# Four-direction selective scan: tiles of two channels by 512 tokens become tiles of one channel by 1024 tokens

## The chip, the cores and the metric

The kernel runs on one core of a Trainium2 chip. A core has five engines with queues of their own: TensorE (PE, with its weight loads PEld), VectorE (DVE), ScalarE (ACT), GpSimd (POOL) and SyncE (SP), which here issues all DMAs. The metric is the device time of one execution in microseconds, lower is better.

## The reference, cut to what matters

The program is four layers of a vision network on a batch of B = 4 images with 96 channels of 64 x 64 pixels: a convolution with a selective scan in four directions (layer 0), an inverted-bottleneck convolution (layer 1), a spectral mixing layer with a feed-forward (layer 2), and linear attention with a feed-forward (layer 3). Nearly all of the time lies in the scan of layer 0, and the change touches that alone. Its core:

```python
K, N, R, DIN, DI = (4, 16, 6, 96, 192)      # directions, states, rank, channels in, channels
L = h * w                                   # 4096 tokens
xs = jnp.stack([xf, xt, jnp.flip(xf, -1), jnp.flip(xt, -1)], axis=1)
xdbl = jnp.einsum('bkdl,ked->bkel', xs, sel_w)
dts_r = xdbl[:, :, :R]
Bs = xdbl[:, :, R:R + N]
Cs = xdbl[:, :, R + N:]
delta = jax.nn.softplus(jnp.einsum('bkrl,kdr->bkdl', dts_r, dt_w) + dt_b[None, :, :, None])
A = -jnp.exp(A_logs.astype(jnp.float32)).reshape(K, DI, N)
def step(hst, inp):
    ut, dt_, bt, ct = inp
    dA = jnp.exp(dt_[..., None] * A[None])
    hst = hst * dA + (dt_ * ut)[..., None] * bt[:, :, None, :]
    y = jnp.einsum('bkdn,bkn->bkd', hst, ct)
    return (hst, y)
```

So for each image and direction there are 192 channels x 16 states = 3072 recurrences along 4096 tokens: decay exp(delta A), input delta u B, then the state times C, summed over the 16 states.

## The kernel before, in words

**Tiling.** The tokens are cut into NCH = 8 chunks of CH = 512. A step is one image, one direction and one chunk, 128 steps in all; its chunks run backwards in directions 2 and 3. A step has PC = 12 units. A unit takes 64 channels and 4 states: its 128 partitions are 32 channel pairs x 4 states, and its free dimension is 2 channels x 512 tokens (index e in the code). `PASSES` is ((0, 1), (2,)): first the channel groups 0 and 1, for each of the NJ = 4 groups of states, then group 2. So there are 1536 units.

**One unit** goes through these functions of `scans`:

- `inputs` (L1264): GpSimd multiplies `rep_g` (delta times u, every channel repeated over 4 partitions) with B (the first half of the tile `rep_BC`, broadcast over e) into a tile `db`, 128 x 1024.
- `decays` (L1268): for e = 0 and 1, ScalarE takes exp of `rep_d` times a column of A into a PSUM bank `da` (128 x 512). There are four such banks, two units' worth. Ahead of each exp stands the state copy `keep` (L1292) of the unit two slots back.
- `states` (L1278): DVE runs two scans of 512 tokens (L1285), from the state kept by the same unit of the step before, or from 0.0 in a direction's first step. In a unit listed in `POOL_C` the scans write an SBUF tile `hc`, otherwise they write over `da`. In the latter case two DVE products with C (L1290) follow, into `hc`.
- `product` (L1304): for a unit of `POOL_C`, (1, 3, 5, 7, 10) of 12, GpSimd copies the last states (L1302) and multiplies `hc` in place with C (L1306), two slots after the scan.
- `sums` (L1319): for two units together PE adds up the 4 states with four matmuls onto the quarters of a PSUM bank `y` (L1330), four slots after the second unit. `sums_out` (L1339) copies the bank by ScalarE (L1344) and stores it.

**What sets the order.** Everything in `scans` stands in an order written by hand for all five engines. The loop over slots (L1361), one unit a slot, emits in this order: loads of coming tiles, pending stores (`flush`), the exp of the next unit, the copy of a finished `y`, GpSimd's input of the unit after next, GpSimd's product of the unit two slots back, this unit's scans and products, the sums that are due, and then side work. Side work is all the rest of the network, cut into streams of small steps with estimated costs (`WORK`, `SHARE`, `RATE`); `advance` (L1451) gives each slot as much of it as its budget allows, in program order behind the slot's scan. `need` (L1245) makes sure that the inputs of the next step are traced, and runs side steps at once by `force` (L1470) until they are. When the scans are over, the streams that are left run alone, with all eight PSUM banks (`alone`, L1489).

**Inputs from DRAM.** `scan_inputs` (L578) computes delta (L610 to L623, stored from `z`), delta times u (L619, stored from `g`) and B, C (stored from `xd`) for each chunk and writes them to DRAM (`d_delta`, `d_du`, `d_bc`). `LOADS` (L1252) says at which unit each tile of the next step is loaded, repeated over partitions: three `rep_d`, three `rep_g`, four `rep_BC` a step, each of 512 KB with runs of 4 KB. `SCAN` gives the numbers of buffers: 3, 3, 5, and 4 `db`, 7 `hc`.

**Around it.** `turn` (L629) and `scan_outputs` (L671) read the results `d_y` once `scanned` says that enough chunks are through; `scan_outputs` ends in L736 and L738, and the convolution of layer 1 (`conv_block`, L742) follows it, chunk pair by chunk pair. For the last image the last direction is 2, backwards, so its chunks are finished in the order 7 to 0, and layer 1 starts while the scan still runs. Side work takes its SBUF tiles from rings: `tmp` (TMP = 10 tiles) and `arrival` (IN = 5).

Of the kernel before, what the change touches and what calls it, by code (L numbers as in the profile page):

```python
# [19 lines left out]
F32 = mybir.dt.float32  # L20
# [8 lines left out]
L = H * W  # L29
# [5 lines left out]
NCH = L // CH  # L35
RPC = CH // W
# [7 lines left out]
SCAN = {"rep_d": 3, "rep_g": 3, "rep_BC": 5, "db": 4, "hc": 7}  # L44
POOL_C = (1, 3, 5, 7, 10)
LAST = {"tab": 24, "more": 6}
TMP, IN = 10, 5

PC = NI * NJ // 2
PAIRS = K * NCH * PC  # L50

# [44 lines left out]
def hybrid_kernel(ctx: ExitStack, tc: tile.TileContext, a: dict):  # L96
# [16 lines left out]
    BANKS = {"mm": 3, "da": 4, "y": 1}  # L113
# [6 lines left out]

    def bank(tag="mm", turn=True):

        if alone and tag == "mm" and turn:
            tag = turns(alone)
        if tag == "mm":
            held_banks[0] += 1
        return psum.tile([128, CH], F32, name=f"ps_{tag}", tag=tag, bufs=BANKS[tag])

# [60 lines left out]
    def pair(tag):  # L189
        return sp.tile([128, 2, CH], F32, name=tag, tag=tag, bufs=SCAN[tag])  # L190

# [25 lines left out]

    d_delta = [images(f"delta{k}_", [NCH, DI, CH], sets=3) for k in range(K)]
    d_du = [images(f"du{k}_", [NCH, DI, CH], sets=3) for k in range(K)]
    d_bc = [images(f"bc{k}_", [NCH, 2 * NS, CH], sets=3) for k in range(K)]  # L220

    d_y = [images(f"y{k}_", [NCH, 256, CH]) for k in range(K)]
# [353 lines left out]
    def scan_inputs(b, u, o, c, done):  # L578
# [16 lines left out]
        for e in (0, 1):  # L595
            later(d_bc[o + 2 * e][i][c], xd[64 * e : 64 * e + 2 * NS])
        for part in range(3):
            yield pe(0.9, 1, part > 0)
            p = bank()
            if part < 2:  # L600
                mm(p, lhsT=dtw[:, o + 2 * part, 0:128], rhs=xd, start=True, stop=True)  # L601
                at = [(slice(0, 128), o + 2 * part, slice(0, 128))]
# [16 lines left out]
            nc.vector.tensor_mul(split(g), split(p), view(ub if part == 2 else ua, o, c))  # L619
            for rows, k, ch in at:  # L620
                later(d_du[k][i][c][ch], g[rows])
# [3 lines left out]
            for rows, k, ch in at:  # L625
                later(d_delta[k][i][c][ch], z[rows])
# [44 lines left out]
    def scan_outputs(b, done):  # L671
# [3 lines left out]
        def fetch(c):  # L675
            out = []
            yt, y0, y2 = (of[b % 2][c] for of in (d_yt, d_y[0], d_y[2]))
            for part in (yt[:128], y2[:128], yt[128:], y2[128:]) + ((y0[128:],) if b == B - 1 else ()):
                s = arrival("ypart")
                load(s[: part.shape[0]], part)  # L680
                out.append(s[: part.shape[0]])
# [508 lines left out]
    PASSES = ((0, 1), (2,))  # L1190
# [17 lines left out]
    def scans(stages):  # L1208
# [8 lines left out]
        for b in range(B):  # L1217
            for k in KORDER[b]:
                for n in range(NCH):
                    steps.append({"b": b, "k": k, "c": NCH - 1 - n if k >= 2 else n, "n": n, "BC": {}, "d": {}, "g": {}})  # L1220
        units = []
        for number, step in enumerate(steps):
            step["at"] = number % (K * NCH)
# [8 lines left out]
        def load_states(step, j):  # L1232
            t = pair("rep_BC")
            of = d_bc[step["k"]][step["b"] % 3][step["c"], 8 * j : 8 * j + 8].rearrange("(s e) l -> s (e l)", e=2)
            load(t.rearrange("p e l -> p (e l)"), of.unsqueeze(0).to_broadcast([32, 4, 2 * CH]))
            step["BC"][j] = t

        def load_channels(step, i, name):
            t = pair(f"rep_{name}")
            of = (d_delta if name == "d" else d_du)[step["k"]][step["b"] % 3][step["c"], 64 * i : 64 * i + 64]  # L1240
            load(t.rearrange("p e l -> p (e l)"),
                 of.rearrange("(p e) l -> p (e l)", e=2).unsqueeze(1).to_broadcast([32, 4, 2 * CH]))
            step[name][i] = t

        def need(step):  # L1245

            while (step["k"] % 2, step["c"]) not in traced[step["b"]]:
                force(stages)
# [394 lines left out]
```

## Time and profile before

| | |
|---|---|
| median of 3 runs | 6344.4 us (6340.63 to 6344.61) |
| profiled execution | 6358.61 us |
| its span, first to last instruction | 6356.8 us |
| first scan, last scan | about 81 us, about 5912 us |
| DMA | 1100.47 MB, mean 173 GB/s, 54.3% of 16 engines' span |

The slices of the span, 40 equal parts of 159 us, a digit being tenths of busy time:

```profile
PE   6732767756888776686469878767898777679998
DVE  4979898998999989989989998888999999889245
ACT  5743777765666677877546656767666667666435
POOL 4857878779999899987899998898999988889100
```

A line of instruction groups in this document reads: code line, engine, operation, output<-inputs with shapes, count, then busy us in total and mean ns of one, then the engine's idle time just before them and which instruction ended it ("<-"). A line of the order of time reads: start in us, length in us (of all instructions merged into the line, their number behind the x), engine, code line, operation. A line of busy time by stretch gives the stretch and its length, then the busy us (and instructions) of PE, PEld, DVE, ACT and POOL, and then the granted TensorE clock, the share of the DMA engines and GB/s.

### The profile page before, as it was taken

The page shows a single profiled execution, that of the slowest core. Times are in us where ns is not written, and L with a number is a line of the kernel's source. Part 1 is how long each engine was busy: PE and PEld are TensorE (multiplying, and loading weights), DVE is VectorE, ACT ScalarE, POOL GpSimd, SP SyncE. Part 2 cuts the span into 40 slices and gives each one's busy share as a digit, 9 for nine tenths or more (in the row PEclk, how much of TensorE's full clock was granted, in tenths as well). Part 3 has the DMA queues.
Part 4 walks back from the last instruction along what each step waited for, and adds up shares of the span by engine and source line. Part 5 has one row for each costly group of instructions (what it writes and reads, how often), then busy time and mean ns, then how long its engine had stood idle before and what let it go on. Part 6 is the DMA issues. An engine that isn't in the chain of part 4 may idle for free. (4 is left out here: it accounts for less than half of the span.)

```text
span 6356.8 us, 84759 instructions
## 1 busy us (share of the span) xinstructions
PE 4685.7 (74%) x27692; PEld 1723.3 (27%) x27692; DVE 5490.6 (86%) x6059; ACT 4191.3 (66%) x8072; POOL 5169.6 (81%) x2743
## 2 busy tenths in 40 slices
PE   6732767756888776686469878767898777679998
PEld 2100212201222642121012236321222552112274
DVE  4979898998999989989989998888999999889245
ACT  5743777765666677877546656767666667666435
POOL 4857878779999899987899998898999988889100
PEclk9855978867998888797779987878899887789999
DMA  5654565667754554456776445456754554566201
GB/s 178 206 167 146 190 204 187 201 201 221 221 162 151 183 181 156 151 193 208 212 213 197 156 152 192 157 162 199 225 171 159 171 192 141 172 209 202 84 13 39
DMA packets 430397, 1100.47 MB, mean 173 GB/s; under 512 B 74138, under 2 KB 75904, under 8 KB 428804
## 3 DMA queue, kind: packets, MB, share of 16 engines
q1 hardware_dynamic: 429956, 1095.06, 54.3%
q8 instruction: 220, 3.60, 0.2%
q14 instruction: 221, 1.81, 0.1%
HBM read 861.88 MB, written 237.44 MB: 173 GB/s over the span
## 5 line engine op out<-in xcount | busy, mean ns | idle before, releaser
L1266 POOL TENSOR_TENSOR db<-rep_g,rep_BC 128x1024 f32<-128x1024 f32 x1536 | 3607.0, 2365 | 689.1 <-DVE hc L1285 323.5
L1276 ACT ACTIVATE ps_da<-rep_d,aneg 128x512 f32<-128x512 f32 x3072 | 2061.8, 690 | 478.8 <-DVE hc L1285 347.2
L1285 DVE TENSOR_TENSOR_SCAN ps_da<-ps_da,state,db 128x512 f32<-128x512 f32 x1568 | 1923.9, 1272 | 274.3 <-ACT state L1300 151.4
L1306 POOL TENSOR_TENSOR hc<-hc,rep_BC 128x1024 f32<-128x1024 f32 x640 | 1511.2, 2361 | 49.3 <-DVE hc L1285 4.5
L1285 DVE TENSOR_TENSOR_SCAN hc<-ps_da,state,db 128x512 f32<-128x512 f32 x1120 | 1371.7, 1266 | 71.3 <-issue 20.6
L1330 PE MATMUL ps_y<-hc,cst 128*32 128x512 f32 x6144 | 1014.4, 739 | 566.2 <-POOL hc L1306 261.1
L1290 DVE TENSOR_TENSOR hc<-ps_da,rep_BC 128x512 f32<-128x512 f32 x1792 | 1135.5, 675 | 0.0
L1300 ACT COPY state<-ps_da 128x1 f32<-128x1 f32 x1568 | 246.3, 157 | 456.9 <-DVE hc L1290 455.4
L1330 PEld LDWEIGHTS ps_y<-hc,cst 128*32 128x32 f32 x6144 | 145.8, 118 | 1210.5 <-issue 438.2
L810 PE MATMUL ps_mm<-h,wd 128*32 128x512 f32 x3120 | 357.0, 593 | 7.0 <-ACT r L155 7.0
L550 PE MATMUL ps_mm<-xp,taps 128*128 128x512 f32 x576 | 294.7, 656 | 54.9 <-ACT ua L552 15.1
L1285 DVE TENSOR_TENSOR_SCAN ps_da<-ps_da,db 128x512 f32<-128x512 f32 x224 | 261.3, 1212 | 39.5 <-ACT state L1300 24.7
L787 PE MATMUL ps_mm<-wd,w 128*32 128x512 f32 x1984 | 254.9, 630 | 29.3 <-DMA wd<-x 20.0
L601 PE MATMUL ps_mm<-xd,dtw 128*128 128x512 f32 x256 | 168.5, 751 | 73.6 <-ACT z L623 53.5
L791 ACT ACTIVATE h<-ps_mm 128x512 f32<-128x512 f32 x261 | 151.8, 597 | 66.5 <-PE ps_mm L787 64.5
L869 PE MATMUL ps_mm<-r,cst 128*128 128x512 f32 x222 | 152.3, 778 | 56.5 <-ACT acc L892 14.2
L616 DVE SCALAR_TENSOR_TENSOR ps_mm<-ps_mm,z 128x512 f32<-128x512 f32 x192 | 131.7, 686 | 70.8 <-ACT z L614 67.0
L1285 DVE TENSOR_TENSOR_SCAN hc<-ps_da,db 128x512 f32<-128x512 f32 x160 | 186.2, 1204 | 6.1 <-issue 3.1
L655 PE MATMUL ps_mm<-ya,cst 128*64 128x512 f32 x192 | 183.1, 1044 | 10.4 <-ACT acc L892 10.4
L610 ACT ACTIVATE z<-ps_mm 128x512 f32<-128x512 f32 x192 | 114.1, 595 | 111.7 <-PE ps_mm L601 59.2
L982 PE MATMUL ps_mm<-wa,xp 128*64 128x96 f32 x1728 | 134.9, 318 | 64.6 <-DVE d L987 61.9
L550 PEld LDWEIGHTS ps_mm<-xp,taps 128*128 128x128 f32 x576 | 115.9, 208 | 229.5 <-issue 159.9
(348 smaller groups left out, 6675.9 us busy)
## 6 DMA issues: line engine op xcount, KB each, us to landing
rep_BC<-bc SPq DMA_DIRECT2D x512, 512.0 KB
rep_g<-du SPq DMA_DIRECT2D x384, 512.0 KB
rep_d<-delta SPq DMA_DIRECT2D x384, 512.0 KB
y<-yt SPq DMA_DIRECT2D x512, 128.0 KB
du<-g SPq DMA_DIRECT2D x128, 256.0 KB
delta<-z SPq DMA_DIRECT2D x128, 256.0 KB
tab<-in_etab SPq DMA_DIRECT2D x112, 256.0 KB
ya<-y SPq DMA_DIRECT2D x24, 1024.0 KB
```

Source lines behind the costliest of these rows:

```text
L550: mm(p, lhsT=taps[:, t, 0:128], rhs=window(t, c + e), start=t == 0, stop=t == 8)
L601: mm(p, lhsT=dtw[:, o + 2 * part, 0:128], rhs=xd, start=True, stop=True)
L655: mm(split(p[:64]), lhsT=const("two")[:, :64], rhs=t[:, :L].rearrange("p (w h) -> p h w", h=H)[:, c * RPC : (c + 1) * RPC, :], start=True, ...
L787: mm(p[32 * n : 32 * n + 32], lhsT=w1[:, 32 * g : 32 * g + 32], rhs=xin[:, n : n + 15 : 2, 1 : W + 1], start=True, stop=True)
L810: mm(p[32 * n : 32 * n + 32], lhsT=held["wd"][:, groups[i], o, dx, :], rhs=here[i][:, :, dx : dx + W], start=dx == 0, stop=dx == 2)
L1266: nc.gpsimd.tensor_mul(x["db"], x["step"]["g"][x["i"]], both(x["step"]["BC"][x["j"]][:, 0]))
L1276: act(x["da"][e], x["step"]["d"][x["i"]][:, e], AF.Exp, scale=aneg[:, av : av + 1])
L1285: nc.vector.tensor_tensor_scan(x["h"][e][:, order], x["da"][e][:, order], x["db"][:, e, order], start, ALU.mult, ALU.add)
L1290: x["made"] = nc.vector.tensor_mul(x["hc"][:, e], x["h"][e], x["step"]["BC"][x["j"]][:, 1])
L1300: nc.scalar.copy(to[:, e : e + 1], x["h"][e][:, end : end + 1])
L1306: x["made"] = nc.gpsimd.tensor_mul(x["hc"], x["hc"], both(x["step"]["BC"][x["j"]][:, 1]))
L1330: done = mm(y[32 * q : 32 * q + 32], lhsT=const("stack"), rhs=x["hc"][:, e], start=first or (x["pass"] == 0 and x["j"] == 0), stop=last or ...
```

## The change

The unit keeps its 128 x 1024 elements, and there are still 1536 of them, but it is cut otherwise: 32 channels (no pairs) x 4 states on the partitions, and 1024 tokens of one channel on the free dimension. What follows from that:

- A step covers 1024 tokens: 64 steps of PC = 24 units, in three passes of two channel groups. `need` asks for both chunks of a step.
- One exp of 1024 elements writes a tile of two PSUM banks; there are two such tiles instead of four single banks. One scan of 1024 takes the place of two of 512, one DVE product of 1024 that of two.
- The input, the state (in units whose product GpSimd makes) and the product are written in place in one tile `w` from a ring of 8; `db` (4) and `hc` (7) are gone. A `w` tile is free again when the sums of its unit are done.
- `POOL_C` becomes (0, 2, 4, 6, 8, 12, 14, 16, 18, 20) of 24; GpSimd's product stays two slots behind the scan. All state copies are ScalarE's, one column each.
- B and C are loaded as tiles of their own, four of each a step, beside six `d` and six `g`, each with 4 buffers; `LOADS` and `OWN` place these loads anew. The DRAM tensors hold 1024 tokens a row; B and C are no longer interleaved.
- The sums come three slots after the second unit (four before). They still take four matmuls for two units; now the halves of a bank are the two chunks.
- TMP goes from 10 to 9, IN from 5 to 4, the ring of `yt` to 1. `scan_outputs` packs two half loads into one tile.
- When the scans are over, `bank("da")` hands out halves of the two-bank tiles in turn. `force` gives banks back when no stream fits.

The diff, cut to its core:

```diff
-SCAN = {"rep_d": 3, "rep_g": 3, "rep_BC": 5, "db": 4, "hc": 7}
-POOL_C = (1, 3, 5, 7, 10)
+SCAN = {"d": 4, "g": 4, "B": 4, "C": 4, "w": 8}
+POOL_C = (0, 2, 4, 6, 8, 12, 14, 16, 18, 20)
-TMP, IN = 10, 5
-PC = NI * NJ // 2
+TMP, IN = 9, 4
+PC = NI * NJ
-    BANKS = {"mm": 3, "da": 4, "y": 1}
+    BANKS = {"mm": 3, "da": 2, "y": 1}
...
+    def decay_banks():
+        return psum.tile([128, CH2], F32, name="ps_da", tag="da", bufs=BANKS["da"])
...
-    PASSES = ((0, 1), (2,))
+    PASSES = ((0, 1), (2, 3), (4, 5))
...
+        def fetch(step, name, i):
+            t = step[name][i] = wide(name)
+            if name in "BC":
+                lo = 4 * i + (NS if name == "C" else 0)
+                of = d_bc[step["k"]][step["b"] % 3][step["c"], lo : lo + 4].unsqueeze(0)
+            else:
+                of = (d_delta if name == "d" else d_du)[step["k"]][step["b"] % 3]
+                of = of[step["c"], 32 * i : 32 * i + 32].unsqueeze(1)
+            load(t, of.to_broadcast([32, 4, CH2]))
...
-            while (step["k"] % 2, step["c"]) not in traced[step["b"]]:
+            while not traced[step["b"]].issuperset((step["k"] % 2, 2 * step["c"] + e) for e in (0, 1)):
                 force(stages)
...
-        LOADS = {4: [("BC", 0)], 5: [("g", 0)], 6: [("g", 1), ("d", 0)], 7: [("d", 1)], 10: [("BC", 1), ("g", 2)],
-                 11: [("BC", 2), ("d", 2)], PC + 1: [("BC", 3)]}
+        LOADS = {14: [("g", 0)], 15: [("g", 1), ("d", 0)], 16: [("d", 1), ("B", 0)], 18: [("B", 1)], 20: [("B", 2), ("C", 0)],
+                 21: [("C", 1)], 22: [("g", 2), ("B", 3)], 23: [("g", 3), ("d", 2)]}
+        OWN = {0: [("C", 2), ("d", 3)], 2: [("C", 3)], 6: [("g", 4)], 7: [("g", 5), ("d", 4)], 8: [("d", 5)]}
...
         def inputs(x):
-            x["db"] = pair("db")
-            nc.gpsimd.tensor_mul(x["db"], x["step"]["g"][x["i"]], both(x["step"]["BC"][x["j"]][:, 0]))
+            x["w"] = wide("w")
+            nc.gpsimd.tensor_mul(x["w"], x["step"]["g"][x["i"]], x["step"]["B"][x["j"]])
...
+            if last is not None:
+                keep(last)
+            av = (x["step"]["k"] * NI + x["i"]) * NJ + x["j"]
+            x["da"] = decay_banks()
+            act(x["da"], x["step"]["d"][x["i"]], AF.Exp, scale=aneg[:, av : av + 1])
...
+            x["h"] = x["w"] if x["pool"] else x["da"]
+            start = 0.0 if step["n"] == 0 else steps[x["number"] - 1]["last"][:, u : u + 1]
+            nc.vector.tensor_tensor_scan(
+                x["h"][:, order], x["da"][:, order], x["w"][:, order], start, ALU.mult, ALU.add
+            )
             if not x["pool"]:
-                for e in (0, 1):
-                    x["made"] = nc.vector.tensor_mul(x["hc"][:, e], x["h"][e], x["step"]["BC"][x["j"]][:, 1])
+                product(x, nc.vector)
...
+        def product(x, engine):
+            x["made"] = engine.tensor_mul(x["w"], x["h"], x["step"]["C"][x["j"]])
...
-            when = at + 4
+            when = at + 3
```

## The prediction

> **What bounds the kernel now.** I read the page's busy times first, then busy time by stage, then the groups of the scan, then a stretch of the vector engine's order of time, and last what its scans waited for.
>
> ```profile
> PE 4685.7 (74%) x27692; PEld 1723.3 (27%) x27692; DVE 5490.6 (86%) x6059; ACT 4191.3 (66%) x8072; POOL 5169.6 (81%) x2743
> ```
>
> By stage (span, then busy PE, PEld, DVE, ACT, POOL):
>
> ```profile
> 600.00:1500.00 900.00, 591.58 (x1851) 162.62 (x1852) 819.90 (x896) 640.43 (x1218) 729.51 (x388) 0.79 0.61 196
> 1500.00:2000.00 500.00, 418.34 (x2270) 115.45 (x2274) 470.21 (x502) 325.09 (x653) 494.05 (x264) 0.90 0.61 188
> 5915.00:6357.00 442.00, 410.24 (x4134) 231.11 (x4130) 164.20 (x301) 181.13 (x285) 0.00 (x0) 0.98 0.14 43
> ```
>
> The scans run from about 81 to 5912 us. In the first line, a stage with much side work, DVE is busy 91% and POOL 81%: DVE is the bound. In the second POOL is at 99%, yet DVE is at 94%: both bind. The last line is the tail without scans, PE at 93%. The groups of the scan:
>
> ```profile
> L1266 POOL TENSOR_TENSOR db<-rep_g,rep_BC 128x1024 f32<-128x1024 f32 x1536 | 3607.0, 2365 | 689.1 <-DVE hc L1285 323.5 <-DVE ps_da L1285 154.5 <-DMA rep_BC<-bc 116.8
> L1276 ACT ACTIVATE ps_da<-rep_d,aneg 128x512 f32<-128x512 f32 x3072 | 2061.8, 690 | 478.8 <-DVE hc L1285 347.2 <-DVE hc L1290 86.1 <-DMA rep_d<-delta 9.7
> L1285 DVE TENSOR_TENSOR_SCAN ps_da<-ps_da,state,db 128x512 f32<-128x512 f32 x1568 | 1923.9, 1272 | 274.3 <-ACT state L1300 151.4 <-ACT ps_da L1276 51.0 <-POOL db L1266 38.2
> L1306 POOL TENSOR_TENSOR hc<-hc,rep_BC 128x1024 f32<-128x1024 f32 x640 | 1511.2, 2361 | 49.3 <-DVE hc L1285 4.5
> L1290 DVE TENSOR_TENSOR hc<-ps_da,rep_BC 128x512 f32<-128x512 f32 x1792 | 1135.5, 675 | 0.0
> L1300 ACT COPY state<-ps_da 128x1 f32<-128x1 f32 x1568 | 246.3, 157 | 456.9 <-DVE hc L1290 455.4
> L1302 POOL COPY state<-hc 128x2 f32<-128x2 f32 x560 | 105.8, 189 | 0.0
> ```
>
> A mean overstates what an instruction costs its engine, since neighbours overlap. So I take distances between starts (start, us, count behind the x):
>
> ```profile
> 1244.22 0.69 DVE L616 SCALAR_TENSOR_TENSOR ps_mm<-ps_mm,z 128x512 f32<-128x512 f32 x1
> 1244.95 0.69 DVE L619 TENSOR_TENSOR g<-ps_mm,ub 128x512 f32<-128x512 f32 x1
> 1245.55 2.46 DVE L1285 TENSOR_TENSOR_SCAN ps_da<-ps_da,state,db 128x512 f32<-128x512 f32 x2
> 1247.92 1.27 DVE L1290 TENSOR_TENSOR hc<-ps_da,rep_BC 128x512 f32<-128x512 f32 x2
> 1249.10 0.69 DVE L616 SCALAR_TENSOR_TENSOR ps_mm<-ps_mm,z 128x512 f32<-128x512 f32 x1
> ```
>
> Two scans take 2.37, two products 1.18, an instruction after an unrelated one of 0.69 comes after 0.60, but L619, which reads what L616 has just written, comes after 0.73: a dependent neighbour costs 0.13 more. Last, what the scans of L1285 waited for (us, times):
>
> ```profile
>   ACT state L1300: 178.4, 114
>   ACT ps_da L1276: 66.0, 44
>   POOL db L1266: 57.3, 43
>   POOL hc L1306: 33.2, 16
> ```
>
> So DVE waits far longer for a late exp (244 us, 158 times) than for GpSimd (about 100 with 9 for L1302).
>
> [...]
>
> **The change part by part.** There are 1536 units before (128 steps of 12) and after (64 of 24), each of the same elements, and the products are split alike: 640 by GpSimd (P units), 896 by DVE (N units).
>
> *Scans and products on DVE.* One scan of 1024 replaces two. [...] a P unit saves 0.12. [...] But before, the order was scan, scan, product, product, with an instruction between each scan and its product; now the product directly follows its own scan and pays the 0.13. An N unit takes 2.25 + 0.13 + 1.13 = 3.51 against 3.55, saving about 0.05. Sum: 640 x 0.12 + 896 x 0.05 = 77 + 45 = **122 us gained** (from 5 without any fixed part on the scan to 240 without the wait). It lies on the path in all stages, if GpSimd follows.
>
> *GpSimd.* Its operands keep their size, 2.32 between starts. The copies of L1302 go: 560 x 0.27 = 151 us of POOL, of which I count nothing by itself; it lets GpSimd fall from 3.37 to 3.28 us a unit, faster than DVE's 0.08 a unit, so that in the second stage above the gain isn't stopped. The floor, 2176 x 2.32 = 5050 us in a zone of 5831, isn't reached.
>
> *State copies.* All go to ScalarE, one a unit, three steps of four: 1536 x 3/4 = 1152 instead of 1568. The in-place product now waits for that copy; GpSimd's queue behind it holds the inputs of later units, which have two slots of lead. Nothing.
>
> *Exp, and two decay tiles of two banks.* [...] 0.18 less of ACT a unit. But before, DVE could begin after the first half (0.69), and ACT could refill the first bank while DVE used the second. Now a scan waits for the whole 1.12, and the exp for the whole tile. Where ACT is already late, each time costs 0.43 more: 158 x 0.43 = 68. Near misses of today: 158 waits of 1.5 us mean suggest some 45 new ones of about 0.3, 14. Two slots of lighter ACT return 0.2 each time, 32. Net **50 lost** (from -32 to 165).
>
> *Loads.* As many of 512 KB as before (1280). B now leads its use by six slots where rep_BC led by two or three (issued at 10, 11 and 13, used from slot 12), so the 117 us that POOL waited for rep_BC should go; it reached DVE only as part of the 100, **25 gained** (0 to 60). In SP's queue each load sits one slot or two behind the last reader of its buffer, as before; stores queue behind it as they do now.
>
> *Ring w of eight.* It replaces 4 + 7 tiles. GpSimd's input of slot s+2 needs the sums of unit s-6, issued on PE at slot s-2 or earlier; DVE then has its two slots of lead. DVE's waits for ps_y today are 6.7 us in all. Nothing (0 to 30 lost).
>
> *Side buffers.* TMP 10 to 9, IN 5 to 4. Today waits for stores of z or g are about 2 us, but the buffers come round in some 19 us and are held for 15 to 20. **15 lost** (0 to 60).
>
> *Steps of two chunks.* At the start the first loads must wait for the second chunk's inputs (its L619 runs at 85 to 87 us, the first scan at 81), 12 lost; and step 1 needs chunks 2 and 3 by slot 14, where chunk 3 was needed by slot 28: some forced work, 8. At the end chunks 1 and 0 come together, where chunk 1 came 12 units earlier: its L738 stands at 5921, and a chunk takes about 20, so 13 later at most, partly under PE's other work: 8. **28 lost** (5 to 70). Sharing of decay banks in the PE-bound tail: nothing.
>
> Sum: -122 - 25 + 50 + 15 + 28 = -54. The profiled execution took 6358.6 (span 6356.8 and 1.8 around it): 6304.6. The median of the runs is 0.22% lower than that execution, 6344.4: **6290**.
>
> **Rivals.** *The lateness falls*: ACT's 0.18 a unit counts more than the coarser release, -32 instead of +50, and the buffers cost nothing, -15: 6304.6 - 97 = 6208, as a run 6190. For it: 66% busy ACT gets lighter everywhere. Against: most late exps follow an ACT operation that waits for PE, which no lighter exp cures. *Slower*: ACT's whole-tile release becomes the bound. With only the next unit's scan as cover (2.25 for a P unit) the chain of copy, exp and two signals takes about 1.5, so a side operation of 0.6 to 0.8 ahead of it uses up the cover. If one unit in four is late by 0.43, the cost is 384 x 0.43 = 165 instead of 50: 6420, as a run 6405. From about 240 late starts (104 us) the gain is gone. For it: ACT is DVE's main releaser. Against: in the stages with most ACT work DVE has 1.3 us of side work a slot as well. *Gain eaten*: costs at their middle between these, 6344.
>
> **Numbers.** About 0.2% can be told from no change, that is 6332 to 6357. Forecast near 6290 (own range 6240 to 6332): 0.42. Lateness falls: 0.21. Eaten: 0.12. Slower: 0.25. Faster 0.63, same 0.12, slower 0.25. The range leaves a tenth out at either end: 6160 to 6430.
>
> **What would show it.** Right: scans of 1024 with a mean near 2335 ns, products near 1210 starting 2.38 after their scan, exps near 1117, no POOL copies, DVE's busy time about 120 lower, its waits for ACT near 290. Wrong: waits for ACT over 350 (the slower rival) or under 220; POOL waiting for PE's sums; ACT waiting for stores of z; a first scan later than 100 us.

## The result, and the profile after

| | before | after |
|---|---|---|
| median of 5 runs each, on one chip | 6340.63 us (6324.45 to 6344.61) | 6282.76 us (6277.07 to 6299.06) |
| profiled execution, its span | 6358.61, 6356.8 us | 6292.35, 6290.6 us |
| start of the first scan, of the last | 81.2, 5908.6 us | 87.6, 5820.6 us |

The changed kernel takes 0.9922 of the time before (95% interval 0.9908 to 0.9937), 58 us less; the two profiled executions differ by 66, because the one of before lies 18 us above its median and the one of after 10. (The last scan of before starts at 5908.6, not at about 5912.) The page of the kernel after, its busy times (compare the first line shown of before):

```profile
PE 4637.2 (74%) x27628; PEld 1718.8 (27%) x27628; DVE 5400.7 (86%) x3627; ACT 3837.2 (61%) x6056; POOL 5073.3 (81%) x2183
```

DVE has 2432 instructions fewer and is busy 90 us less. By stage (span, then busy PE, PEld, DVE, ACT, POOL):

```profile
600.00:1500.00 900.00, 618.36 (x1936) 167.34 (x1936) 826.31 (x563) 608.92 (x964) 743.14 (x320) 0.80 0.63 202
1500.00:2000.00 500.00, 411.30 (x2360) 119.45 (x2360) 467.50 (x279) 294.52 (x460) 495.08 (x214) 0.91 0.58 185
5824.00:6290.00 466.00, 423.97 (x4124) 235.80 (x4116) 161.48 (x302) 180.99 (x289) 0.00 (x0) 0.96 0.14 42
```

What bounds the kernel is the same as before. DVE is at 92% and GpSimd at 83% in the stage with much side work, and GpSimd is at 99%, DVE at 93%, in the second. It is the same work in less time, not another bound. The tail is 22 us longer. The groups of the scan, after (busy us, mean ns, then the idle time before them):

```profile
L1272 POOL TENSOR_TENSOR scan_w<-scan_g,scan_B 128x1024 f32<-128x1024 f32 x1536 | 3606.6, 2373 | 452.8 <-PE ps_y L1324 358.3 <-DMA scan_B<-bc 80.9 <-DMA scan_C<-bc 5.5
L1279 ACT ACTIVATE ps_da<-scan_d,aneg 128x1024 f32<-128x1024 f32 x1536 | 1715.5, 1117 | 533.5 <-DVE scan_w L1286 273.6 <-DVE scan_w L1301 238.1 <-DVE gn L537 2.4
L1286 DVE TENSOR_TENSOR_SCAN ps_da<-ps_da,state,scan_w 128x1024 f32<-128x1024 f32 x672 | 1575.9, 2345 | 197.9 <-ACT ps_da L1279 175.1 <-ACT state L1298 15.9 <-POOL scan_w L1272 4.1
L1301 POOL TENSOR_TENSOR scan_w<-scan_w,scan_C 128x1024 f32<-128x1024 f32 x640 | 1516.3, 2369 | 285.9 <-ACT state L1298 175.6 <-DVE scan_w L1286 94.7 <-DMA delta<-z 10.2
L1301 DVE TENSOR_TENSOR scan_w<-ps_da,scan_C 128x1024 f32<-128x1024 f32 x896 | 1097.3, 1225 | 71.6 <-DMA scan_C<-bc 3.6 <-DVE ps_da L1286 0.5 <-PE ps_mm L1018 0.4
```

Exp 1117, scan 2345 and product 1225 ns are close to the sizes that the prediction named (1117, 2335, 1210). Beside 690, 1272 and 675 for the same with 512 elements in the kernel before, the 512 elements more took 427, 1073 and 550 ns. The last line has 71.6 us of idle time of which the releasers named explain under 5: this is the product waiting some 0.08 us, 896 times, for the scan just ahead of it. In DVE's order of time (start, length):

```profile
1247.97 2.35 DVE L1286 TENSOR_TENSOR_SCAN ps_da<-ps_da,state,scan_w 128x1024 f32<-128x1024 f32 x1
1250.36 1.23 DVE L1301 TENSOR_TENSOR scan_w<-ps_da,scan_C 128x1024 f32<-128x1024 f32 x1
1251.50 1.03 DVE L634 TENSOR_TENSOR g<-ps_mm,ua 128x512 f32<-128x512 f32 x1
1252.44 2.34 DVE L1286 TENSOR_TENSOR_SCAN scan_w<-ps_da,state,scan_w 128x1024 f32<-128x1024 f32 x1
1254.69 0.68 DVE L631 SCALAR_TENSOR_TENSOR ps_mm<-ps_mm,z 128x512 f32<-128x512 f32 x1
```

The product begins 2.39 after its scan, 0.04 after the scan's end; where no product follows, the next instruction begins 2.25 after the scan, before it has ended. What the scans of L1286 waited for, by the releaser that the profile names (us, times):

```profile
  ACT ps_da L1279: 292.9, 234
  ACT state L1298: 35.5, 23
  POOL scan_w L1272: 12.8, 10
  POOL scan_w L1301: 3.9, 3
```

By these names DVE's waits for ScalarE rose from 244 (158 times) to 328 us (257 times), and its waits for GpSimd fell from 100 to 17. The names are not safe, though. In the kernel before, this scan had its input since 648.78, and the profile names no releaser for its 1.16 us of idle time ("issue"); ScalarE's two exps for it begin at 654.80:

```profile
655.59 2.46 DVE L1285 TENSOR_TENSOR_SCAN hc<-ps_da,state,db 128x512 f32<-128x512 f32 x2 [1.16 <-issue]
```

```profile
654.80 1.30 ACT L1276 ACTIVATE ps_da<-rep_d,aneg 128x512 f32<-128x512 f32 x2
```

An exp of 0.69 that begins at 654.80 ends at 655.49, just before the scan begins. So every scan was paired with its own exp and its own input (the n-th scan with the n-th exp, 3072 of each before, 1536 after; no scan starts before the exp and the input so assigned have ended). Whenever a scan followed idle time, its own exp or input had ended either less than 0.13 us before the scan's start or more than 0.25 us before it, so it is clear which of the two, if either, it had waited for:

| idle time of DVE before scans, us (times) | before | after |
|---|---|---|
| own exp ended last | 334 (219) | 335 (264) |
| own input from GpSimd ended last | 41 (35) | 4 (3) |
| neither | 14 (9) | 7 (6) |

In sum the waits for late exps did not rise; more scans wait, each for less. Of the 39 waits before that had no name (38 us) 38 were for the own exp, and so were 25 of the 62 put down to GpSimd. Below, "by name" is what the profile names and "own exp", "own input" are these pairs. GpSimd itself now waits for two things that it hardly waited for before (us, times, longest):

```profile
POOL scan_w L1272 <- PE ps_y L1324: 358.3, 151, 9.1
POOL scan_w L1301 <- ACT state L1298: 175.6, 120, 6.4
```

**Where the 66 us went.** For every DVE instruction between the first and the last scan I took the distance to the next start, less the idle time that the order of time shows there. That splits the whole stretch without overlaps:

| us | before | after | difference | prediction |
|---|---|---|---|---|
| scans of the 640 units of GpSimd | 1523.9 | 1447.7 | -76 | -77 |
| scans and products of the 896 units of DVE | 3171.7 | 3178.2 | +6 | -45 |
| side instructions | 624.3 | 670.3 | +46 | 0 |
| DVE idle | 507.6 | 436.8 | -71 | +48 (loads -25, exp +50, buffers +15, forced work 8) |
| first to last scan | 5827.4 | 5733.0 | -94 | -74 |
| start | | | +6 | +12 |
| from the last scan's start to the end | 448.2 | 470.0 | +22 | +8 |

The sum, -94 + 6 + 22 = -66, is the difference of the spans. The total was foreseen to 12 us (-54); four of its terms were off by more than that.

### The profile page after: what moved, and what is told of

Its sections match the earlier page's. It is cut to its first block, busy times and chain, and to the rows that moved or that the text cites. A ratio compares the mean times of both kernels' runs of the same rounds, so it can differ in the third digit from the quotient of the medians.

```text
span 6290.6 us, 78721 instructions
## 1 busy us (share of the span) xinstructions
PE 4637.2 (74%) x27628; PEld 1718.8 (27%) x27628; DVE 5400.7 (86%) x3627; ACT 3837.2 (61%) x6056; POOL 5073.3 (81%) x2183
## 5 line engine op out<-in xcount | busy, mean ns | idle before, releaser
L1272 POOL TENSOR_TENSOR scan_w<-scan_g,scan_B 128x1024 f32<-128x1024 f32 x1536 | 3606.6, 2373 | 452.8 <-PE ps_y L1324 358.3
L1279 ACT ACTIVATE ps_da<-scan_d,aneg 128x1024 f32<-128x1024 f32 x1536 | 1715.5, 1117 | 533.5 <-DVE scan_w L1286 273.6
L1301 POOL TENSOR_TENSOR scan_w<-scan_w,scan_C 128x1024 f32<-128x1024 f32 x640 | 1516.3, 2369 | 285.9 <-ACT state L1298 175.6
L1286 DVE TENSOR_TENSOR_SCAN ps_da<-ps_da,state,scan_w 128x1024 f32<-128x1024 f32 x672 | 1575.9, 2345 | 197.9 <-ACT ps_da L1279 175.1
L1324 PE MATMUL ps_y<-scan_w,cst 128*32 128x512 f32 x6144 | 1005.4, 733 | 561.6 <-ACT yt L1338 207.4
L1301 DVE TENSOR_TENSOR scan_w<-ps_da,scan_C 128x1024 f32<-128x1024 f32 x896 | 1097.3, 1225 | 71.6 <-DMA scan_C<-bc 3.6
L1286 DVE TENSOR_TENSOR_SCAN scan_w<-ps_da,state,scan_w 128x1024 f32<-128x1024 f32 x480 | 1123.4, 2340 | 38.8 <-ACT ps_da L1279 33.4
L1286 DVE TENSOR_TENSOR_SCAN ps_da<-ps_da,scan_w 128x1024 f32<-128x1024 f32 x224 | 511.9, 2285 | 86.3 <-ACT ps_da L1279 67.0
L1324 PEld LDWEIGHTS ps_y<-scan_w,cst 128*32 128x32 f32 x6144 | 148.4, 118 | 1215.6 <-issue 633.3
L1286 DVE TENSOR_TENSOR_SCAN scan_w<-ps_da,scan_w 128x1024 f32<-128x1024 f32 x160 | 364.8, 2280 | 23.9 <-ACT ps_da L1279 17.4
```

The costliest lines, as they stand in the source:

```text
L1272: nc.gpsimd.tensor_mul(x["w"], x["step"]["g"][x["i"]], x["step"]["B"][x["j"]])
L1279: act(x["da"], x["step"]["d"][x["i"]], AF.Exp, scale=aneg[:, av : av + 1])
L1286: nc.vector.tensor_tensor_scan(x["h"][:, order], x["da"][:, order], x["w"][:, order], start, ALU.mult, ALU.add)
L1301: x["made"] = engine.tensor_mul(x["w"], x["h"], x["step"]["C"][x["j"]])
L1324: done = mm(y[32 * q : 32 * q + 32], lhsT=const("stack"), rhs=group[m]["w"][:, e * CH : e * CH + CH], start=first, stop=last)
```

## The experiments

Each run is given as its ratio to the kernel before on the same chip. The changed kernel stands at 0.9922. Waits and busy times come from one profiled execution of each run, which can lie some 20 us off the run's median; a table behind the last experiment says how far.

**1. One exp and two-bank decay tiles, alone, in the kernel before.**

```diff
-    BANKS = {"mm": 3, "da": 4, "y": 1}
+    BANKS = {"mm": 3, "da": 2, "y": 1}
...
+            both_da = decay_banks()
+            act(both_da, x["step"]["d"][x["i"]].rearrange("p e l -> p (e l)"), AF.Exp, scale=aneg[:, av : av + 1])
+            x["da"] = [both_da[:, :CH], both_da[:, CH:]]
```

(The exp takes one column of A for both channels of a pair; the reference gives all channels the same A, so the values are the same.)

> The kernel before with one part of the change alone: two decay tiles of two banks and one exp of 1024 a unit (it uses the first channel's column of A for both channels of a pair, which holds the same values); the two scans of 512 and all else stay. My theory, that the coarser release makes the exp late oftener than the shorter exp makes it early: DVE's waits for ACT rise from 244 to some 320 to 340 us, the span up by 60 to 90 (6405 to 6435 on 6344), of which some 10 lie in the tail, where banks are shared. Rival, the lighter ACT counts more: waits under 220, 20 to 30 us faster.

Measured: 6551.55 us, ratio 1.0336 (1.0323 to 1.0349), far outside. Not for the reason expected: waits for ACT by name rose only from 244 to 285, and for the own exp they did not rise (334 to 329). DVE's order of time shows what did it:

```profile
3440.04 2.59 DVE L1296 TENSOR_TENSOR_SCAN ps_da<-ps_da,state,db 128x512 f32<-128x512 f32 x2
3442.72 1.29 DVE L1301 TENSOR_TENSOR hc<-ps_da,rep_BC 128x512 f32<-128x512 f32 x2
3443.93 2.44 DVE L1296 TENSOR_TENSOR_SCAN hc<-ps_da,state,db 128x512 f32<-128x512 f32 x2
```

Where the scans write back into the shared tile, the pair takes 2.68 to the next start instead of 2.37; where they write `hc` it still takes 2.36. Both halves belong to one tile now. That the second scan therefore waits for the first, and the product for the second, is a reading; what the lines show is the 0.31 us more. By the split above, the units whose product DVE makes took 300 us more, 0.33 each. Not all of it reached the time: DVE's idle time fell by 97, and the profiled execution is 203 longer. In the change one scan covers both banks, so this pair of neighbours isn't there. Because DVE is slower here, the run doesn't tell what the coarser release alone does.

**2. State copies to ScalarE, alone.**

```diff
-                if last is not None and not last["pool"]:
+                if last is not None:
...
-                    nc.gpsimd.tensor_copy(to, x["hc"][:, :, end])
+                    nc.scalar.copy(to, x["hc"][:, :, end])
...
```

> The kernel before with GpSimd's state copies moved to ScalarE. Theory, that GpSimd is not late because of its copies but through its loads and rings: DVE's waits for GpSimd stay at 60 to 100 us, ACT gets 560 more copies of 0.16, the time stays within 0.3% (6325 to 6360). Rival, that the copies of 0.27 us each were what made GpSimd late: waits fall to 20 to 40 us and the time by 40 to 70 (6275 to 6305).

Measured: 6335.23, ratio 0.9996 (0.9988 to 1.0004). GpSimd was busy 92 us less, the scans waited 27 us for their own input in place of 41, side instructions took 13 us more (last section), and the time didn't move. By name DVE's waits for GpSimd fell from 100 to 56: below the 60 to 100 of the theory, above the 20 to 40 of the rival.

**3. Chunks announced in pairs, alone** (what `scan_outputs` may read at the end).

```diff
-            scanned[b] += 1
+            halves[b] += 1
+            if halves[b] % 2 == 0:
+                scanned[b] += 2
```

> The kernel before, but finished chunks are announced to the consumers in pairs, as a step of 1024 tokens does. Theory, that this is what makes the tail longer: from the last scan to the end 445 us become 455 to 470, the rest is unchanged, 6355 to 6370. Rival, that the tail grows through the sharing of banks: tail stays at 445, no change.

Measured: 6341.61, ratio 1.0012 (1.0004 to 1.002). From the last scan's start to the end it took 12 us more. The same stretch is 8 us longer in the first experiment, which has shared banks and no pairs; 12 + 8 gives nearly the 22 of the change. (The stretch takes 448 to 451 us in the four profiles that have neither, 465 to 473 in the eight that have both.) I had put 8 on the pairs and nothing on the banks.

**4. One side buffer less, alone.**

```diff
-TMP, IN = 10, 5
+TMP, IN = 9, 5
```

> The kernel before with 9 side tiles instead of 10. My prediction priced this and IN 4 at 15 us lost: 6350 to 6370, with ACT or DVE waiting for stores of z and g for 10 us or more. Rival, that the ring was long enough: within 0.1%, waits for stores at 2 to 4 us.

Measured: 6338.83, ratio 1.0004 (0.9994 to 1.0014). The 15 us of the prediction aren't there; the other half of that term, `arrival` at 4, wasn't tried.

**5. The changed kernel with DVE's product behind the slot's side work**, to take the dependent neighbour away.

```diff
-            if not x["pool"]:
-                product(x, nc.vector)
...
                 owed -= did
+            if x is not None and not x["pool"]:
+                product(x, nc.vector)
```

> The changed kernel with DVE's product of a unit emitted behind the slot's side work, so that where DVE has side work the product no longer follows its own scan directly. Theory, that the wait of 0.13 us of a dependent neighbour lies on the path: some 45% of the 896 products are parted from their scan, 50 us less on DVE, of which a later release of the decay tile takes back 0 to 40: 6240 to 6280. Rival, the decay tile is what counts: waits for ACT rise from 328 past 400, 6300 to 6340.

Measured: 6274.98, ratio 0.9912 (0.9895 to 0.993): not to be told from 0.9922. Only 288 of the 896 products were parted from their scan (45% were expected), since in the many slots without side work on DVE the product still follows its scan. Scans and products of DVE's units fell by 47 us; DVE's idle time rose by 21. The time lies in the range of the theory, but what of the saving reaches it is below what these runs resolve.

**6. A ring of seven `w`**, in the changed kernel.

```diff
-SCAN = {"d": 4, "g": 4, "B": 4, "C": 4, "w": 8}
+SCAN = {"d": 4, "g": 4, "B": 4, "C": 4, "w": 7}
```

> The changed kernel with the ring w at 7 instead of 8, which takes one slot of lead away. Theory, that GpSimd's 358 us of waiting for PE's sums reach DVE only because two slots of lead hide them: GpSimd's waits for the sums double, DVE's waits for GpSimd rise from 17 to 60 to 150, 6310 to 6400. Rival, there is more lead than needed: DVE's waits for GpSimd under 30, 6275 to 6295.

Measured: 6313.57, ratio 0.9964 (0.9951 to 0.9977): the time of the theory with the waits of the rival. GpSimd's waits for PE's sums rose from 358 to 532 us, but DVE's waits for GpSimd only from 17 to 26, and DVE's idle time stayed the same. Its side instructions took 26 us more. Most of that is one group (this run first, then the changed kernel):

```profile
L914 DVE TENSOR_SCALAR acc<-acc,bq 128x512 f16<-128x512 f16 x96 | 106.3, 1116 | 8.7 <-ACT acc L909 8.2
L914 DVE TENSOR_SCALAR acc<-acc,bq 128x512 f16<-128x512 f16 x96 | 82.5, 868 | 9.4 <-ACT acc L909 8.8
```

This version costs some 27 us, and the part that the trace shows lies in side instructions that take longer (here 1116 ns in place of 868; last section), not in waits for the ring. So the 27 are the price of this version, and can't be called the worth of the eighth tile.

**7. The sums one slot earlier**, in the changed kernel.

```diff
-            when = at + 3
+            when = at + 2
```

> The changed kernel with the sums two slots after the second unit instead of three. Theory, that GpSimd's wait for the sums is hidden: it falls from 358 to under 200, PE waits longer for GpSimd's products (165 to over 250), the time stays within 0.3% (6265 to 6300). Rival, the wait is on the path: 30 to 80 us faster.

Measured: 6310.47, ratio 0.9963 (0.995 to 0.9975), slower than the theory and the rival had it. The wait at the sums went (358 to 82), but GpSimd's in-place product now waited 412 us for the state copy where it had waited 176, and PE's sums waited 242 us for GpSimd's products and 158 for DVE's where they had waited 165 and 73. DVE's idle time from the first scan to the last rose by 28, its waits for the own exp by 11. That PE's longer waits delay what stands behind them, and ScalarE in turn, is a reading and not shown. The run puts other waits in the place of the one that it takes away, so it doesn't tell what the wait for the sums costs by itself.

**8. The changed kernel with B loaded two slots ahead**, about as rep_BC was (two to three).

```diff
-        LOADS = {14: [("g", 0)], 15: [("g", 1), ("d", 0)], 16: [("d", 1), ("B", 0)], 18: [("B", 1)], 20: [("B", 2), ("C", 0)],
-                 21: [("C", 1)], 22: [("g", 2), ("B", 3)], 23: [("g", 3), ("d", 2)]}
-        OWN = {0: [("C", 2), ("d", 3)], 2: [("C", 3)], 6: [("g", 4)], 7: [("g", 5), ("d", 4)], 8: [("d", 5)]}
+        LOADS = {14: [("g", 0)], 15: [("g", 1), ("d", 0)], 16: [("d", 1), ("B", 0)], 20: [("C", 0)],
+                 21: [("C", 1)], 22: [("B", 1), ("g", 2)], 23: [("g", 3), ("d", 2)]}
+        OWN = {0: [("B", 2), ("C", 2), ("d", 3)], 2: [("B", 3), ("C", 3)], 6: [("g", 4)], 7: [("g", 5), ("d", 4)], 8: [("d", 5)]}
```

> The changed kernel with the tiles of B for three of four groups loaded two slots ahead of their first use, as late as before the change, instead of six. Theory, that the loads' lead is what took GpSimd's lateness away: GpSimd waits for these loads 60 us and more beyond the start, DVE's waits for GpSimd rise from 17 to 50 to 100, 6300 to 6350. Rival, the lead does nothing, since a load lands in 5 us: no change.

Measured: 6335.0, ratio 0.9997 (0.9988 to 1.0005). Nearly the whole gain is gone, some 48 us. The profiled execution, 6310.62, is the fastest of the 22 and shows only part of that loss. (In the changed kernel a load of B lands 5.0 us after its issue, in the median of 256.) The edit also changes the order of the loads in SP's queue, which wasn't tried alone.

```profile
L1272 POOL TENSOR_TENSOR scan_w<-scan_g,scan_B 128x1024 f32<-128x1024 f32 x1536 | 3609.0, 2378 | 588.7 <-DMA scan_B<-bc 282.8 <-PE ps_y L1324 270.7 <-DMA tab<-in_etab 5.4
```

GpSimd waited 283 us for B, against 81 in the changed kernel (77 of these are one wait at the start), and the scans waited for GpSimd's input again (63 us for the own input, in place of 4; 327 for the own exp, in place of 335):

```profile
  ACT ps_da L1279: 278.6, 225
  POOL scan_w L1272: 74.4, 52
```

**9. The same lead, alone, in the kernel before.**

```diff
-SCAN = {"rep_d": 3, "rep_g": 3, "rep_BC": 5, "db": 4, "hc": 7}
+SCAN = {"rep_d": 3, "rep_g": 3, "rep_BC": 6, "db": 4, "hc": 7}
...
-        LOADS = {4: [("BC", 0)], 5: [("g", 0)], 6: [("g", 1), ("d", 0)], 7: [("d", 1)], 10: [("BC", 1), ("g", 2)],
-                 11: [("BC", 2), ("d", 2)], PC + 1: [("BC", 3)]}
+        LOADS = {4: [("BC", 0)], 5: [("g", 0)], 6: [("g", 1), ("d", 0), ("BC", 1)], 7: [("d", 1)], 9: [("BC", 2)], 10: [("BC", 3), ("g", 2)],
+                 11: [("d", 2)]}
...
-                yt = sp.tile([128, CH], F32, name="yt")
+                yt = sp.tile([128, CH], F32, name="yt", bufs=1)
```

> The kernel before with one thing of the change: the loads of B and C lead their first use by six slots (all four of a step are issued in the step before it, at units 6, 9 and 10, from a ring of six), with the ring of yt at one to make room. Theory (the longer lead is a main part of the gain, about 48 us in the run with late B): GpSimd's waits for rep_BC, 117 us, go to under 30, DVE's waits for GpSimd fall from 100 to 40-50, and the time falls by 30 to 50 us, 6285 to 6305. Rival (what GpSimd no longer waits for, DVE then waits for at ScalarE, as when the copies alone were taken from GpSimd): DVE's waits for ACT rise from 244 by as much, and the time stays within 10 us of before.

Measured: 6332.29, ratio 0.9998 (0.9987 to 1.0009). GpSimd's waits for rep_BC went from 117 to 12, as both theories had it, and the rival was right on the time. By name DVE's waits for GpSimd fell by 42 and those for ACT rose by 21; the scans waited 11 us for their own input in place of 41, and 351 for their own exp in place of 334. So the lead is needed by the changed kernel, but it is no gain by itself.

**10. Two exps of 512 in the changed kernel.**

```diff
-            act(x["da"], x["step"]["d"][x["i"]], AF.Exp, scale=aneg[:, av : av + 1])
+            for e in (0, 1):
+                half = slice(e * CH, e * CH + CH)
+                act(x["da"][:, half], x["step"]["d"][x["i"]][:, half], AF.Exp, scale=aneg[:, av : av + 1])
```

> The changed kernel with two exps of 512 into the halves of the two-bank tile, in place of one of 1024; the scan still waits for both. It adds 0.18 us of ScalarE to each unit and to each chain from release to scan, and leaves the coarse release. Theory (a late exp is late by the length of ScalarE's chain): each of some 300 late starts gets 0.18 later, 55 us, and near misses add 20: DVE's waits for ACT go from 328 to near 400, and the time to 6340 to 6365. Rival (late exps stand behind side operations that wait for PE, and have room besides): the waits stay under 350, and the time under 6310.

Measured: 6324.93, ratio 0.9992 (0.9978 to 1.0006): some 44 us above the changed kernel, 15 short of what the theory asked and 15 above the rival. The scans' waits, by name:

```profile
  ACT ps_da L1281: 373.8, 281
  POOL scan_w L1272: 20.5, 16
  ACT state L1300: 13.8, 9
```

That is 388 us for ACT in place of 328; for the own exp 412 us (314 times) in place of 335 (264). The theory had put 55 and 20 for near misses, 75 together, and 77 came. It fits the theory's mechanism, that a late exp is late by the length of ScalarE's chain and the single exp shortens every such chain (1.12 us in place of 1.30 for two). (The profiled execution is 20 us above its median; side instructions took 23 us less in it.)

**11. GpSimd's state copies behind the next exp**, in the changed kernel.

```diff
-            if last is not None:
+            if last is not None and not last["pool"]:
                 keep(last)
...
             act(x["da"], x["step"]["d"][x["i"]], AF.Exp, scale=aneg[:, av : av + 1])
+            if last is not None and last["pool"]:
+                keep(last)
```

> The changed kernel with the state copy of GpSimd's units put behind the next exp in ScalarE's order (that copy reads the tile w, so the exp needn't wait for it). Theory (state copies lengthen the chain that ends in a scan): a fifth of 480 chains gets 0.16 to 0.25 shorter, DVE's waits for ACT fall from 328 to near 305, and the time by 10 to 25 us; GpSimd's in-place product waits 1 us longer for the copy (its waits for ACT 176 go over 300), which is hidden as long as DVE's waits for GpSimd stay under 40. Rival (GpSimd has no room where it is busy at 99%): DVE's waits for GpSimd rise by more than the exps gain, and the time is 10 to 30 us longer.

Measured: 6285.12, ratio 0.9924 (0.9903 to 0.9946), no change. Waits for ACT came to 327 us, where 305 were expected, and GpSimd's wait for the copy to 241, hidden: DVE waited 9 us for GpSimd. These 480 copies of 0.19 ahead of the exp aren't what makes exps late; the interval of the time, some 14 us either way, leaves room for a gain smaller than that.

**12. GpSimd's share of the products by step**, in the changed kernel.

```diff
+POOL_MORE, POOL_FEW = tuple(range(0, 24, 2)), (0, 2, 5, 8, 10, 13, 16, 18, 21)
...
-                                      "pool": u in POOL_C})
+                                      "pool": u in (POOL_MORE if number in MORE else POOL_FEW if number in FEW else POOL_C)})
```

> The changed kernel with GpSimd's share of the products set step by step from the profile: 12 of 24 in the 27 steps in which GpSimd was busy at most 86%, 9 in the 19 in which it was busy 98% or more, 10 in the other 18 as before. Theory (in the first kind DVE's own work is the bound, in the second GpSimd's): a product takes 1.27 us of DVE's path and 2.32 of GpSimd's. The first kind gives up to 27 x 2 x 1.27 = 69 us, half of which I expect to reach the end, the second 19 x 2.32 = 44, less what DVE takes on, 25: the time falls by about 60 us, to 6225. Rival (in both kinds waits for ScalarE and PE take up what is freed): 6260 to 6285.

Measured: 6247.95, ratio 0.9871 (0.9848 to 0.9893), the fastest version, some 32 us below the change (60 were expected, the rival had 0 to 20). Step by step against the profile of the change, the 27 steps in which GpSimd took 12 products became 54 us shorter in all (69 at most were to be had), the 19 in which it took 9 became 6 longer, the others stayed. So the first half of the theory holds better than I expected, and the second fails: where GpSimd is at 99%, DVE is at 93%, and what it takes over from GpSimd presumably costs it as much as GpSimd's relief gives.

**All profiled executions side by side** (us; times in brackets). The first column is the distance of the profiled execution from the run's median; the last counts the DVE instructions that lasted more than 4 us.

| run | off its median | own exp | own input | DVE idle | side instructions | over 4 us |
|---|---|---|---|---|---|---|
| before | +18 | 334 (219) | 41 | 508 | 624 | 0 |
| 1 one exp | +10 | 329 (210) | 10 | 411 | 622 | 0 |
| 2 copies to ScalarE | -4 | 322 (221) | 27 | 474 | 638 | 5 |
| 3 pairs | 0 | 321 (214) | 40 | 486 | 619 | 0 |
| 4 one `tmp` less | +8 | 335 (217) | 40 | 501 | 619 | 0 |
| 9 lead alone | +9 | 351 (233) | 11 | 493 | 621 | 0 |
| after | +10 | 335 (264) | 4 | 437 | 670 | 4 |
| 5 product later | -4 | 305 (242) | 4 | 458 | 675 | 7 |
| 6 ring of seven | +12 | 331 (261) | 9 | 438 | 696 | 8 |
| 7 sums earlier | +1 | 346 (268) | 4 | 465 | 663 | 6 |
| 8 B late | -24 | 327 (260) | 63 | 470 | 658 | 3 |
| 10 two exps | +20 | 412 (314) | 3 | 509 | 648 | 3 |
| 11 copy behind exp | -17 | 326 (256) | 5 | 417 | 668 | 6 |
| 12 share by step | -8 | 343 (258) | 2 | 444 | 662 | 3 |

## Why the prediction came out right, step by step

The number was right: 6290 predicted, 6282.76 measured. The steps below it were right in part, and that the sum came so near was luck: DVE's own work came out about 97 us dearer than predicted, its idle time 119 us lower, and the two cancelled.

- **Scans of GpSimd's units: right.** -76 measured, -77 predicted. Two scans took 2.37 from the first start to the next instruction; for one of 1024 the prediction put 2.25, and it came to 2.26. What it put for the elements of the longer scan was the author's estimate, which no trace of before shows; so were the product of 1024 (1.13 from start to start, 1.15 came) and the exp (1.12, and 1.117 came).
- **Scans and products of DVE's units: the term that failed small.** "An N unit takes 2.25 + 0.13 + 1.13 = 3.51 against 3.55". The unit takes 3.55 after, 3.54 before: scan to product is 2.40 and product to next 1.15 in the mean, two hundredths more each than I took. A saving of 0.05 was the difference of two sums each uncertain by that much, and multiplied by 896 it looked like 45 us. The dependent neighbour (2.40 to the product in place of 2.26, 0.14 us) eats the whole saving. If the lines of the first experiment are read as above, two such neighbours cost 0.31 there.
- **Side instructions: put at nothing, without a reason given.** They took 46 us more in nearly the same number (861 for 865). 37 of these are in three groups with operands in SBUF alone (last section).
- **Loads: too small for what hangs on it, and not a term.** "25 gained": taken out of the change the lead is worth about 48 us, put into the kernel before it is worth nothing. GpSimd's waits for it did go, as predicted. As a term of a sum it has no one value.
- **Exp: the two effects were there, the net was wrong.** Net +50 was predicted, with waits for ACT "near 290" by name, and they came to 328 by name. But the names had hidden part of these waits before: for the own exp they were 334 before and 335 after, a net of +1. Experiment 10 measures the return of the shorter exp by taking it away: 77 us in waits, where the prediction counted 32. If the two effects add up, the coarser release cost about 78, near the 82 (68 + 14) that it was priced at; this remainder wasn't measured alone. So the mis-sized term is the return, which was counted for the 158 late exps that the profile names, at 0.2 each; by pairs 219 were late before.
- **State copies, ring w, sums: the zeros.** Copies alone are worth nothing (0.9996), as predicted. The ring was "nothing (0 to 30 lost)"; a wait of GpSimd for PE's sums was named as a sign that the prediction was wrong, and it came, 358 us, but DVE waits only 17 us for GpSimd. GpSimd runs ahead of DVE, and most of its waits didn't reach DVE. Whether eight tiles are more than is needed stays open, since the 27 us of experiment 6 don't lie in waits.
- **Side buffers: not found in the half that was tried.** 15 predicted, nothing measured with one `tmp` less; fewer `arrival` tiles weren't tried alone.
- **Start and tail: the sum nearly right, the parts not.** The start took 6 instead of 12. The tail took 22 instead of 8: 12 by the pairs of chunks, about 8 by the shared banks, which had been put at nothing.
- **The idle time: wrong in sign.** I had +48 for what waits do, and DVE's idle time fell by 71. The scans' waits for their own input fell by 37, their other waits by 7, those for their own exp rose by 1: -43. The other 28 fell at side instructions and products. No single part put in alone frees this time: copies, lead and one side buffer less are each worth nothing in the kernel before, while taking out the shorter exp costs 44 in the changed kernel and taking out the longer lead 48.

Of the rivals, the slower one decided at waits for ACT over 350 and the faster one at under 220, both by name; 328 lies between them, and by pairs these waits didn't move, so neither mechanism is what happened (the faster one's other half, buffers at nothing, held for `tmp`). The slower one's chain of copy, exp and two signals, "about 1.5", was the author's estimate; of DVE's waits for the exp by name in the changed kernel, 83 last 1.25 or 1.26 us, more than of any other length. **What stays open** is why the lead is worth so much in the changed kernel and nothing before. One reading is that a scan has two late releasers and that taking one away shows the other: in experiment 9 the own input gave back 30 us and the own exp took 17 of them, and the changed kernel moved several things at once. No run here removes two together in the kernel before.

## What to carry to other kernels

Merging two scans into one saved 0.12 us a unit here (2.38 to 2.26, means of 640) where no dependent product came next, and nothing where the merge put that product directly behind its scan (3.54 before, 3.55 after): look at what stands between producer and consumer before and after, and don't trust a saving that is smaller than the uncertainty of its two sums. Don't take the named releaser of a wait for its cause: pair each instruction with its own producers, and see which of them ended last. Price waits together: here the wait for late loads, removed from the old kernel, was worth nothing, and put back into the finished one it cost most of the gain; test a part by taking it out of the new kernel as well as by putting it into the old one. And when one engine's share of the work was set for the whole run, set it by stage: here giving GpSimd more in the stages where it had room brought 54 us.

## What the runs showed of the hardware

**A small DVE instruction between two SBUF operands took 7.42 us in place of 0.25 while GpSimd worked.** In the changed kernel, DVE's order of time (first fence) and GpSimd's at the same moment:

```profile
4200.85 0.23 DVE L1128 TENSOR_TENSOR vk<-vk,ps_mm 96x96 f32<-96x96 f32 x1
4201.10 7.42 DVE L1135 TENSOR_TENSOR vk<-vk,cst 96x96 f32<-96x96 f32 x1
4208.45 2.34 DVE L1286 TENSOR_TENSOR_SCAN ps_da<-ps_da,state,scan_w 128x1024 f32<-128x1024 f32 x1
```

```profile
4194.52 9.30 POOL L1272 TENSOR_TENSOR scan_w<-scan_g,scan_B 128x1024 f32<-128x1024 f32 x4
4203.75 2.37 POOL L1301 TENSOR_TENSOR scan_w<-scan_w,scan_C 128x1024 f32<-128x1024 f32 x1
4206.04 2.37 POOL L1272 TENSOR_TENSOR scan_w<-scan_g,scan_B 128x1024 f32<-128x1024 f32 x1
4211.22 2.35 POOL L1272 TENSOR_TENSOR scan_w<-scan_g,scan_B 128x1024 f32<-128x1024 f32 x1 [2.81 <-PE ps_y L1324]
```

L1128, with one operand in PSUM, takes 0.23. L1135, of the same shape with both in SBUF, takes 7.42 and ends at 4208.5, as GpSimd's row of products ends at 4208.4. The shortest of its four takes 0.25. Why it lasts until GpSimd's row ends is not shown. Such a lengthening is called a stop below. Two products of one row, 1x96, in the same kernel: 9.91 together at 2006 us behind four such operations, 0.71 in the tail without GpSimd:

```profile
2006.42 9.91 DVE L1012 TENSOR_TENSOR d<-d,rib 1x96 f32<-1x96 f32 x2
```

```profile
6032.53 0.71 DVE L1012 TENSOR_TENSOR d<-d,rib 1x96 f32<-1x96 f32 x2
```

The scans' products with one operand in PSUM keep their length beside GpSimd (1223 to 1229 ns, all 896). Most of these stops are short: of the 42 DVE instructions in the changed kernel that took over 1 us longer than the shortest of their kind, 36 took at most 2.5 us, about one GpSimd operation. By groups, L1012 went from 20.3 to 38.2 us, L1135 from 3.9 to 15.7, L914 (f16 to f16, both in SBUF) from 75.2 to 82.5 between the two kernels, together 37 of the 46 us of side work (in the kernel before these lines are L995, L1118 and L897). These sums vary from version to version of the changed kernel (L1012 between 21 and 47), so part of each is chance.

**The stops that outlast one GpSimd operation came when GpSimd lost its state copies.** In the kernel before and in the four runs of it that leave these copies with GpSimd, no DVE instruction lasts over 3 us. In experiment 2, whose only edit gives the copies to ScalarE, five last over 4 us, and in the changed kernel and its versions 3 to 8 each. The products of one row, L995 in the kernel before, with the shortest, median and longest duration in ns, before (first line) and in experiment 2:

```profile
L995 DVE TENSOR_TENSOR d<-d,rib x16: 335/1511/2380, 2053.2 to 6108.1; 1x96 f32<-1x96 f32 x16
L995 DVE TENSOR_TENSOR d<-d,rib x16: 333/679/6569, 2043.4 to 6080.9; 1x96 f32<-1x96 f32 x16
```

So a copy of 0.19 us between GpSimd's long operations went along with shorter stops of DVE, though it is no gain by itself: experiment 2 has 13 us more of side work and the same time. Why the copies do this, and what makes up the rest of the 46 us, is not shown.
